# Convolution taps of six of eight value head pairs split over ScalarE, VectorE and GpSimd, with silu one pair of projections later

## The chip, the cores and the metric

The kernel runs on one core of one Trainium2 chip. The metric is the device time of one execution in microseconds (us). Five engines matter here, each with its own instruction queue that runs in order: TensorE (PE; its weight loads are shown as PEld), VectorE (DVE), ScalarE (ACT), GpSimd (POOL), and SyncE (SP), whose queue issues nearly all DMAs. GpSimd works on SBUF; results of matmuls lie in PSUM and are read by VectorE and ScalarE.

## The reference

The block is an adaptive layernorm around a gated delta-rule attention layer, followed by a mixture of experts. The input has 4 batches, 1024 tokens and 256 channels; the attention has 16 heads of 64 channels (C = 1024). Only the part that makes the values matters for this change; keys and queries are made in the same way.

```python
def _causal_conv(x, w, b):      # K = 4 taps per channel, causal
    y = jax.lax.conv_general_dilated(x, w, window_strides=(1,), padding=[(K - 1, 0)],
            feature_group_count=C, dimension_numbers=('NCH', 'OIH', 'NCH'))
    return y + b[None, :, None]
v = jnp.einsum('btd,cd->bct', hidden_states, Wv)
v = jax.nn.silu(_causal_conv(v, conv_v_w, conv_v_b))
...
def step(S, xs):                # a scan over the tokens
    kt, vt, qt, at, bt = xs
    v_old = jnp.einsum('bhij,bhj->bhi', S, kt)
    upd = vt - at[..., None] * v_old
    dS = upd[..., :, None] * kt[..., None, :]
    S = jnp.clip(at[..., None, None] * S + bt[..., None, None] * dS, -5.0, 5.0)
    ot = jnp.einsum('bhij,bhj->bhi', S, qt)
    return (S, ot)
...
g = jax.nn.silu(jnp.einsum('btd,cd->btc', hidden_states, Wg) + bg)
y = y * g
```

So each value channel is a projection of the normed rows, then o[t] = b + sum over j of w[j] * x[t + j - 3], then silu. The gate g is a second projection with a silu of its own, and multiplies the attention's output.

## The kernel before

All data is float32. The 1024 tokens are cut into 32 chunks of 32 tokens, and two chunks make a pair (class `Pair`). A tile of one head pair for one pair of chunks has 128 partitions (two heads of 64 channels) and 256 elements (2 chunks x 4 batches x 32 tokens); there are eight head pairs (HP = 8).

The main part is a software pipeline over the 16 pairs. While pair g's two chunks go through the recurrence (`passes`, L1098: state S, outputs, the output projection), pair g+1 is prepared: norm, decays, keys and queries, values and gates, the triangular system. Each of these jobs is a Python generator, and `work` (L1350) steps the generators in the order of the string `PLAN` (L59), one letter a step: `k` keys and queries, `v` values, `c` passes, `b` bounds, `d` decays, `t` triangle, `s` scaling, `r` routing, and so on; what is left of the generators after the string is run to its end in the order of the dictionary. The order in which the program is written out in this way is the order on PE, DVE, ACT and POOL (a hand-made schedule); semaphores between the engines are derived from what each instruction reads and writes. After the 16 pairs come the experts (`blocks`), from about 1600 us of the span on.

`values` (L760) makes, for each two head pairs (hp even): two projections of two matmuls each (`project`, L606, matmuls at L610) into two of three PSUM banks, which all short-lived products share in turn (`bank`, L401); ScalarE then writes tap 0 and the bias from PSUM to the tile `v` (L619). `convolve` (L624) adds taps 1, 2 and 3 on VectorE, one SCALAR_TENSOR_TENSOR each (L628), so six for the two head pairs; a bank is free when the third has read it. Then come the two gate projections (L780) with their silu on ScalarE into `gate` (L787), and, in the step after the second, the silu of the 512 elements of `v` (L634). These are six steps `v` for two head pairs, and 24 for a pair, as many as `PLAN` has.

Lines that the prediction's steps touch:

- L1231 (`decayed`): aS = S * last decay, on GpSimd, 128 x 1024, four times a pair of chunks; L1196 (`state`): S = ps_s + aS on VectorE.
- L1304, L1312, L1319 (`bounds`): on VectorE, a small product, a transpose, and two scans of 128 x 32 that read two tiles of SBUF.
- L726 (`decays`): two scans of 128 x 512 that read two tiles of SBUF; L705: sigmoid into ab_r on ScalarE, with a table load before it.
- L533 (`routing`): the matmul of the router, into a bank; L853 (`triangle`): the products of keys with keys and queries.
- L1001 (`scaled`): GpSimd multiplies keys and queries by a scale that a DMA brings; L1278: x1 = x1 + add on GpSimd; L934 to L956: VectorE's products and sums of the triangular inverse.
- L1019 (`below`): matmuls of the next step; L1252: yT = ps_y * gate on VectorE, which frees two banks.

The steps around the second value convolution stand in `PLAN` as `... c22 v7 v8 v9 c23 x c24 c25 c26 k28 b5 k29 c27 c28 b6 k30 r1 c29 ...` (the number says which step of its generator it is). c22 ends with L1196, v9 is the convolution of head pairs 2 and 3, c23 issues L1231, b5 is L1304 and L1312, b6 is the two L1319, k30 the last convolution of keys and queries, c29 the next L1196.

Of the kernel before, what the change touches and what calls it, by code (L numbers as in the profile page):

```python
# [36 lines left out]
ALU = mybir.AluOpType  # L37
# [3 lines left out]
B, D, C, NH, DH, KC = 4, 256, 1024, 16, 64, 4  # L41
HP = NH // 2
TC, TH, TE = 32, 16, 8
# [138 lines left out]
def adaln_block(ctx: ExitStack, tc: tile.TileContext, a: dict, out: bass.AP):  # L182
# [16 lines left out]
    n_safe = cst.tile([1, 3], I32, name="n_safe")  # L199
    rt = Routes(nc, cst, nch, con, ones, modt)  # L200
    chunks(tc, a, nch, con, ones, modt, modc, x1_dram, rt, out)
    blocks(tc, a, nch, con, rt, out)
    with tc.tile_pool(name="n_ps", bufs=1, space=PSUM) as pp:
# [158 lines left out]
def chunks(ctx, tc, a, nch, con, ones, modt, modc, x1_dram, rt, out):  # L362

    nc = tc.nc
# [16 lines left out]
    is_open, done = {}, set()  # L381

    def take(pool, shape, name, tag=None, bufs=1, **more):
        tag = tag or name
        assert is_open.get(tag, 0) < bufs, tag
        is_open[tag] = is_open.get(tag, 0) + 1
        if bufs > 1:
            more["bufs"] = bufs
        return pool.tile(shape, F32, name=name, tag=tag, **more)
# [6 lines left out]
    def need(*what):  # L396
        assert done.issuperset(what), what
# [3 lines left out]
    def bank(shape, name):  # L401
        banks[0] += 1
        return ps_g.tile(shape, F32, name=name, tag=f"g{banks[0] % 3}")
# [9 lines left out]
    QC, KK, VC = 0, 1, 2  # L413
# [17 lines left out]
    def load_v(hp):  # L431
        w = s3.tile([P, 2, P], F32, name="w_v", bufs=3)
        nc.sync.dma_start(w, a["w_qkv"][:, :, VC, hp])
        wg = s3.tile([P, 2, P], F32, name="w_gt", bufs=4)
        for p in range(2):
            nc.sync.dma_start(wg[:, :, half_p(p)], a["w_g"][:, :, p, hp * DH : (hp + 1) * DH])
        return w, wg
# [168 lines left out]
    def project(w, h_t, x, hp, o):  # L606

        ps = bank([P, 2 * B, KC - 1 + TC], "ps_q")
        for dc in range(2):
            nc.tensor.matmul(  # L610
                ps.rearrange("p y t -> p (y t)"),
                lhsT=w[:, dc],
                rhs=h_t[:, dc].rearrange("p x b t -> p (x b t)"),
                start=(dc == 0),
                stop=(dc == 1),
            )
        taps = conv[:, x, hp]
        o = o.rearrange("p x b t -> p (x b) t")
        nc.scalar.activation(  # L619
            o, ps[:, :, 0:TC], AF.Identity, scale=taps[:, 0:1], bias=taps[:, KC : KC + 1]  # L620
        )
        return ps, taps, o

    def convolve(*projected):  # L624

        for j in range(1, KC):
            for ps, taps, o in projected:
                nc.vector.scalar_tensor_tensor(  # L628
                    o, ps[:, :, j : j + TC], taps[:, j : j + 1], o, op0=ALU.mult, op1=ALU.add
                )  # L630

    def silu(f):
        f = f.rearrange("p h x b t -> p (h x b t)")
        nc.scalar.activation(f, f, AF.Silu)  # L634
# [5 lines left out]
    class Pair:  # L640
# [100 lines left out]
        def keys_and_queries(self):  # L741
            need(("h", self.g), ("halo", self.g))
            kq = self.kq = take(s2, [P, 2, HP, 2, B, TC], "kq", bufs=2)
            for hp in range(HP):
                w = w_next.pop(0)
                w_next.append(load_kq((hp + 2) % HP))
                two = []
                for x, i in ((KK, 0), (QC, 1)):
                    two.append(project(w[:, :, i], self.h_t, x, hp, kq[:, i, hp]))
                    yield  # L750
                convolve(*two)
                yield
                if hp % 2:
                    for i in range(2):
                        silu(kq[:, i, hp - 1 : hp + 1])
                        if i and hp == HP - 1:
                            done.add(("kq", self.g))
                        yield

        def values(self):  # L760

            need(("h", self.g), ("halo", self.g))
            self.v = []
            gate = self.gate = take(s2, [P, HP, 2, B, TC], "gate", bufs=2)
            for hp in range(HP):
                if hp % 2 == 0:
                    two, wgs = [], []
                    self.v.append(take(s2, [P, 2, 2, B, TC], "v", bufs=6))
                    for i in range(2):
                        w, wg = v_next.pop(0)  # L770
                        v_next.append(load_v((hp + i + 2) % HP))
                        wgs.append(wg)
                        two.append(project(w, self.h_t, VC, hp + i, self.v[-1][:, i]))
                        yield
                    convolve(*two)
                    yield
                wg = wgs[hp % 2]
                ps = bank([P, 2 * B, TC], "ps_gt")
                for dc in range(2):
                    nc.tensor.matmul(  # L780
                        ps,
                        lhsT=wg[:, dc],
                        rhs=self.h_t[:, dc, :, :, KC - 1 :].rearrange("p x b t -> p (x b) t"),
                        start=(dc == 0),
                        stop=(dc == 1),
                    )
                nc.scalar.activation(  # L787
                    gate[:, hp].rearrange("p x b t -> p (x b t)"),
                    ps.rearrange("p y t -> p (y t)"),
                    AF.Silu,  # L790
                    bias=b_gt[:, hp : hp + 1],
                )
                yield
                if hp % 2:
                    silu(self.v[-1])
                    if hp == HP - 1:
                        done.add(("v", self.g))
                    yield

        def rows_of_k(self):  # L800

            need(("kq", self.g), ("dec", self.g))
            kend = self.kend = []
            kmax = take(s1, [P, 32], "kmax")
            for par in range(2):
                kend.append(take(s3, [P, HP, 2, DH], "kend", bufs=3))
                for x in range(2):
                    need(("kq", self.g))
                    hs = slice(4 * x, 4 * x + 4)
                    ps = bank([P, 4, 2, DH], "ps_kt")  # L810
                    for i in range(4):
                        nc.tensor.transpose(
                            ps[:, i].rearrange("q p j -> q (p j)"),
                            self.kq[:, 0, 4 * x + i, par].rearrange("q b t -> q (b t)"),
                            ident,
                        )
                    pick = lambda z: z.rearrange("q (p x h) -> q x h p", p=2, x=2)[:, par, hs]
                    nc.vector.tensor_reduce(pick(kmax), ps, AX.X, ALU.max)
                    nc.vector.tensor_tensor(
                        kend[par][:, hs],  # L820
                        ps,
                        pick(self.dec[:, :, TC - 1]).unsqueeze(3).to_broadcast([P, 4, 2, DH]),
                        ALU.mult,
                    )
                    yield
            done.add(("kt", self.g))

            nc.vector.tensor_scalar_max(kmax, kmax, -SILU_MIN)
            self.k_twice = take(s2, [P, 2, 32], "k_twice", bufs=3)
            in_halves(self.k_twice, kmax)  # L830
            close("kmax")
            yield
            k_t = s1.tile([P, 2, TC], F32, name="k_t")
            nc.vector.transpose(
                k_t.rearrange("p x t -> p (x t)"), self.k_twice.rearrange("p x n -> p (x n)")
            )
            nc.sync.dma_start(of_pair(1, self.g), k_t.rearrange("p x t -> p (x t)"))
            yield
# [666 lines left out]
    for g in range(npair):  # L1505
# [4 lines left out]
        if g + 1 < npair:  # L1510
            x = newer
# [895 lines left out]
```

## Time and profile before

| what | us |
|---|---|
| median of three runs | 1913.18 |
| lowest and highest of them | 1906.1 and 1915.0 |
| the profiled execution, its own time | 1922.9 |
| its span, first to last instruction | 1921.1 |
| busy in the span: PE, DVE, ACT, POOL | 1632.0, 1482.3, 826.7, 716.4 |
| granted TensorE clock, mean over the span | 0.919 |
| one SCALAR_TENSOR_TENSOR of `v`, L628 (384 of them) | 0.476 |
| tap 0 of `v` on ACT, L619 (128 of them) | 0.573 |
| silu of `v` on ACT, L634 | 0.62 |
| one L1001 on POOL, 128 x 512 (128 of them) | 1.299 |
| one L1231 on POOL, 128 x 1024 (64 of them) | 1.914 |

The span is from the first to the last instruction of the profiled execution, which took 1922.9 us by its own measure; the medians come from other executions. In the stretch from 150 to 1420 us fourteen pairs of chunks go by, 90.7 us each; there PE is busy for 1132.5 of 1270 us, DVE for 1044.7, ACT for 613.5 and POOL for 493.2. Durations of single instructions include their start-up: instructions that follow each other on one engine overlap a little, so that six L628 in a row take 2.43 to 2.53 us and not 2.86.

### The profile page before, as it was taken

What the parts mean: (1) busy time and instruction counts of PE and PEld (TensorE: products, weight loads), DVE (VectorE), ACT (ScalarE), POOL (GpSimd) and SP (SyncE); (2) the same over time, 40 slices, a digit from 0 to 9 for tenths busy, and PEclk for the clock granted to TensorE, in tenths of its full rate; (3) what the DMA queues carried; (4) which work ended last, traced back from release to release, by engine and by line L of the source; (5) the groups of instructions that cost most, each with busy time, mean ns of one, the idle gap of its engine ahead of it and who ended that gap; (6) DMA issues with size and microseconds to landing.
All of it is one profiled execution on the core that took longest, in us unless ns stands there. A gap on an engine that the chain in (4) does not pass through costs nothing.

```text
span 1921.1 us, 88201 instructions
## 1 busy us (share of the span) xinstructions
PE 1632.0 (85%) x38610; PEld 1297.1 (68%) x38610; DVE 1482.3 (77%) x3622; ACT 826.7 (43%) x1652; POOL 716.4 (37%) x913
## 2 busy tenths in 40 slices
PE   5578999889989898989898989898888675989994
PEld 3456676667676766767676767676667564878883
DVE  4678797968788888878787978797968335789973
ACT  3344545444545544545445444554443112334331
POOL 1032343424342525252534343433424432454343
PEclk9889998989999998989899989998989677999997
DMA  4455444443545445354535453636343216788882
GB/s 117 127 161 129 105 108 94 107 109 95 148 115 141 123 120 137 107 134 111 146 103 150 106 153 97 161 94 153 110 112 112 56 36 207 187 208 219 231 231 35
DMA packets 431490, 249.52 MB, mean 130 GB/s; under 512 B 242996, under 2 KB 410808, under 8 KB 430840
## 3 DMA queue, kind: packets, MB, share of 16 engines
q1 hardware_dynamic: 416488, 223.65, 43.6%
q0 software_dynamic: 13664, 18.38, 5.2%
q8 instruction: 306, 5.01, 1.1%
q10 hardware_dynamic: 944, 1.77, 0.3%
q14 instruction: 88, 0.72, 0.1%
HBM read 165.99 MB, written 81.87 MB: 129 GB/s over the span
## 4 chain that ended last, share of the span: by engine, by line
PE 66%; DVE 11%; issue 7%; POOL 5%; SPq 5%; DMA 4%; ACT 3%; POOLq 0%; DVEq 0%; ACTq 0%
PE ps_q L610 22%; PE ps_hm L2116 6%; PE ps_yb L2129 6%; PE ps_w L1265 5%; PE ps_gt L780 4%; PE ps_u L1149 3%; PE ps_kk L853 3%; PE ps_o L1208 2%; PE ps_z L1127 2%; SPq L423 2%; PE ps_t L1031 2%; PE ps_s L1187 2%; DMA sc<-g_scratch 2%; PE ps_t L1019 2%; DVE kq L628 2%
## 5 line engine op out<-in xcount | busy, mean ns | idle before, releaser
L628 DVE SCALAR_TENSOR_TENSOR kq<-ps_q,w_conv,kq 128x256 f32<-128x256 f32 x768 | 319.7, 476 | 150.2 <-ACT kq L619 149.6
L610 PE MATMUL ps_q<-hT,w_kq 128*128 128x280 f32 x1024 | 323.2, 460 | 58.9 <-issue 20.6
L610 PEld LDWEIGHTS ps_q<-hT,w_kq 128*128 128x128 f32 x1024 | 203.5, 213 | 125.9 <-issue 58.2
L619 ACT ACTIVATE kq<-ps_q,w_conv 128x256 f32<-128x256 f32 x256 | 142.4, 563 | 234.8 <-PE ps_q L610 233.1
L1001 POOL TENSOR_TENSOR kq<-kq,sc 128x512 f32<-128x512 f32 x128 | 163.5, 1299 | 143.6 <-DMA sc<-g_scratch 116.5
L2136 POOL DMA_INDIRECT out<-yb,at_b x72 | 120.4, 1672 | 190.2 <-DVE gate L2106 48.7
L628 DVE SCALAR_TENSOR_TENSOR v<-ps_q,w_conv,v 128x256 f32<-128x256 f32 x384 | 158.9, 476 | 41.9 <-ACT v L619 41.7
L1231 POOL TENSOR_TENSOR aS<-S,last 128x1024 f32<-128x1024 f32 x64 | 122.5, 1914 | 135.9 <-DVE S L1196 133.4
L780 PE MATMUL ps_gt<-hT,w_gt 128*128 128x256 f32 x512 | 144.3, 410 | 29.6 <-issue 20.5
L787 ACT ACTIVATE gate<-ps_gt,b_gt 128x256 f32<-128x256 f32 x128 | 60.5, 473 | 239.3 <-PE ps_gt L780 239.1
L610 PE MATMUL ps_q<-hT,w_v 128*128 128x280 f32 x512 | 153.5, 441 | 11.6 <-issue 4.7
L2116 PE MATMUL ps_hm<-hT,w 128*128 128x256 f32 x576 | 136.4, 392 | 7.6 <-issue 5.9
L2123 ACT ACTIVATE hm<-ps_hm,b 128x256 f32<-128x256 f32 x144 | 68.2, 474 | 167.5 <-issue 120.4
L2129 PE MATMUL ps_yb<-w,hm 128*128 128x256 f32 x576 | 130.3, 379 | 0.0
L2116 PEld LDWEIGHTS ps_hm<-hT,w 128*128 128x128 f32 x576 | 112.7, 197 | 25.9 <-issue 8.9
L610 PEld LDWEIGHTS ps_q<-hT,w_v 128*128 128x128 f32 x512 | 97.7, 204 | 47.3 <-issue 13.1
L780 PEld LDWEIGHTS ps_gt<-hT,w_gt 128*128 128x128 f32 x512 | 92.0, 194 | 53.1 <-issue 28.5
L1265 PE MATMUL ps_w<-w_o,yT 128*128 128x256 f32 x512 | 121.0, 391 | 4.3 <-DVE yT L1252 2.8
L1278 POOL TENSOR_TENSOR x<-x,add 128x256 f32<-128x256 f32 x32 | 29.0, 905 | 236.4 <-DVE add L1276 232.3
L2129 PEld LDWEIGHTS ps_yb<-w,hm 128*128 128x128 f32 x576 | 106.7, 190 | 13.4 <-DVE yb L2134 0.3
L1265 PEld LDWEIGHTS ps_w<-w_o,yT 128*128 128x128 f32 x512 | 98.2, 195 | 20.1 <-DVE yT L1252 3.0
L619 ACT ACTIVATE v<-ps_q,w_conv 128x256 f32<-128x256 f32 x128 | 71.3, 573 | 93.7 <-PE ps_q L610 93.7
(265 smaller groups left out, 3230.5 us busy)
## 6 DMA issues: line engine op xcount, KB each, us to landing
w<-in_w SPq DMA_DIRECT2D x72, 512.0 KB
rows_scratch<-zero_row SPq DMA_DIRECT2D x272, 132.0 KB
w_kq<-in_w_qkv SPq DMA_DIRECT2D x260, 128.0 KB
sc<-g_scratch SPq DMA_DIRECT2D x128, 256.0 KB
w_v<-in_w_qkv SPq DMA_DIRECT2D x130, 128.0 KB
w_gt<-in_w_g SPq DMA_DIRECT2D x260, 64.0 KB
u_scratch<-u SPq DMA_DIRECT2D x128, 128.0 KB
hb<-rows_scratch SPq DMA_DIRECT2D x36, 264.0 KB
```

The lines of the kernel that those rows point to most:

```text
L610: nc.tensor.matmul(ps.rearrange("p y t -> p (y t)"), lhsT=w[:, dc], rhs=h_t[:, dc].rearrange("p x b t -> p (x b t)"), start=(dc == 0), sto ...
L619: nc.scalar.activation(o, ps[:, :, 0:TC], AF.Identity, scale=taps[:, 0:1], bias=taps[:, KC : KC + 1])
L628: nc.vector.scalar_tensor_tensor(o, ps[:, :, j : j + TC], taps[:, j : j + 1], o, op0=ALU.mult, op1=ALU.add)
L780: nc.tensor.matmul(ps, lhsT=wg[:, dc], rhs=self.h_t[:, dc, :, :, KC - 1 :].rearrange("p x b t -> p (x b) t"), start=(dc == 0), stop=(dc == 1),
L787: nc.scalar.activation(gate[:, hp].rearrange("p x b t -> p (x b t)"), ps.rearrange("p y t -> p (y t)"), AF.Silu, bias=b_gt[:, hp : hp + 1],)
L1001: nc.gpsimd.tensor_tensor(o, o, sc[:, h4 : h4 + 4], ALU.mult)
L1231: nc.gpsimd.tensor_tensor(aS.rearrange("q b h i -> q (b h) i"), S[:, bs].rearrange("q b h i -> q (b h) i"), self.pair.last[self.par][:, bs ...
L1265: nc.tensor.matmul(ps_w, lhsT=self.yT[:, hp].rearrange("q b t -> q (b t)"), rhs=w_o[:, hp], start=(hp == 0), stop=(hp == HP - 1),)
L2116: nc.tensor.matmul(ps, lhsT=self.w1[:, dc, fc * P : (fc + 1) * P], rhs=self.hT[:, dc], start=(dc == 0), stop=(dc == 1),)
L2123: nc.scalar.activation(self.hm[:, fc], ps, AF.Gelu, bias=self.b1[:, fc : fc + 1])
L2129: nc.tensor.matmul(ps, lhsT=self.hm[:, fc, s * P : (s + 1) * P], rhs=self.w2[:, fc], start=(fc == 0), stop=(fc == 3),)
L2136: return nc.gpsimd.indirect_dma_start(out=places, out_offset=bass.IndirectOffsetOnAxis(ap=self.at[:, s : s + 1], axis=0), in_=y, in_offset ...
```

## The change

For head pairs 0 to 5 (hp = 0, 2, 4) the four taps are made on two engines: ScalarE writes tap 0 and the bias into `v` as before, and then tap 1 into a second place, `more`, with a second instruction (`half_taps`); VectorE adds taps 2 and 3 to `more`, two instructions for each head pair in place of three; GpSimd adds `more` to `v`, one instruction of 128 x 512 for two head pairs. `more` is the place of the gates of the next two head pairs in the tile `gate`, which is written by its own silu later. The last two head pairs (hp = 6) stay as they were.

The silu of `v` moves: where that of head pairs 2 and 3 stood, that of 0 and 1 is issued, and so on; the first place is empty, and that of the last two head pairs is issued in a 25th step, after the end of `PLAN`. In a pair of chunks there are six more instructions on ACT, six fewer on DVE, and three more on POOL. No DMA and no matmul is added, removed or moved.

```diff
-    def convolve(*projected):
-
-        for j in range(1, KC):
+    def convolve(*projected, first=1):
+
+        for j in range(first, KC):
             for ps, taps, o in projected:
                 nc.vector.scalar_tensor_tensor(
                     o, ps[:, :, j : j + TC], taps[:, j : j + 1], o, op0=ALU.mult, op1=ALU.add
                 )
+
+    def half_taps(w, h_t, hp, o, more):
+
+        ps, taps, o = project(w, h_t, VC, hp, o)
+        nc.scalar.mul(more, ps[:, :, 1 : 1 + TC], taps[:, 1:2])
+        return ps, taps, more
...
-                        two.append(project(w, self.h_t, VC, hp + i, self.v[-1][:, i]))
+                        o = self.v[-1][:, i]
+                        if hp + 2 < HP:
+                            more = gate[:, hp + 2 + i].rearrange("p x b t -> p (x b) t")
+                            two.append(half_taps(w, self.h_t, hp + i, o, more))
+                        else:
+                            two.append(project(w, self.h_t, VC, hp + i, o))
                         yield
-                    convolve(*two)
+                    if hp + 2 < HP:
+                        convolve(*two, first=2)
+                        flat = lambda z: z.rearrange("p h x b t -> p (h x b t)")
+                        o = flat(self.v[-1])
+                        nc.gpsimd.tensor_tensor(o, o, flat(gate[:, hp + 2 : hp + 4]), ALU.add)
+                    else:
+                        convolve(*two)
                     yield
...
                 if hp % 2:
-                    silu(self.v[-1])
-                    if hp == HP - 1:
-                        done.add(("v", self.g))
+                    if hp > 1:
+                        silu(self.v[-2])
                     yield
+            silu(self.v[-1])
+            done.add(("v", self.g))
+            yield
```

## The prediction

> **What bounds the kernel now.** I read the page first, then the waits of the stretch from 150 to 1420 us (fourteen of the fifteen pairs that run beside a recurrence), then the timelines of each engine over the pair that begins at 843 us. The page's first table and its chain of waits:
>
> ```profile
> PE 1632.0 (85%) x38610; PEld 1297.1 (68%) x38610; DVE 1482.3 (77%) x3622; ACT 826.7 (43%) x1652; POOL 716.4 (37%) x913
> ...
> PE 66%; DVE 11%; issue 7%; POOL 5%; SPq 5%; DMA 4%; ACT 3%; POOLq 0%; DVEq 0%; ACTq 0%
> ```
>
> PE carries two thirds of the chain, DVE a ninth. So time saved on DVE counts only where PE stands and waits for DVE. The waits of the stretch name such places:
>
> ```profile
> DVE S L1196 <- POOL aS L1231: 15.4, 10, 2.9
> ...
> PE ps_q L610 <- DVE yT L1252: 14.5, 9, 2.8
> ...
> PE ps_t L1019 <- ACT ab_r L705: 12.0, 11, 1.1
> ...
> PE ps_l L533 <- DVE kq L628: 3.2, 13, 0.2
> ```
>
> The columns are us in total, times, longest. Line 2 is the end of a pair: PE waits for yT, which stands behind the last L1196 on DVE, and that waits for GpSimd's aS (line 1) in ten pairs, 4 to 13. Line 4 is small, but it happens in every pair. PE is at the convolution's heels there, so any delay of that convolution is a delay of PE.
>
> **The three convolutions that change**, for the pair at 843 us. In a queue that is full, L628 follows L628 every 0.394 us (five take 2.05, and the last 0.475: (2.05 - 0.475) / 4). Two fewer save DVE 0.79 us. The new ACT instruction is nearest to L2102 of the experts, a multiply of 128 x 256 by a column, 0.497 us; L619 with a bias column takes 0.573. I take 0.50, of which 0.40 follows an instruction before it.
>
> First (863.9 to 867.5 us). ACT's two instructions for the two heads start 0.95 us apart, as PE delivers them. The new one fits behind the first, but the second head's ends at 865.79, so DVE, which is not late here, ends at 867.10 instead of 867.47. What follows waits for ACT's tap 0 of kq at 868.96, as before. ACT's copies of z come 0.40 later; PE, busy until 866.31, waits under 0.2 us for them and had 0.29 idle just behind. Worth: 0, within 0.2 us.
>
> Third (908.9 to 914.3). DVE is late here (it starts at 911.89, ACT ended at 910.45), so the full 0.79 us is saved, and then stands as idle time in front of the last L1196, which waits 0.89 us for aS already. aS comes from a queue of SP's DMAs and GpSimd work that the change leaves alone. Worth: 0 in pairs 4 to 13.
>
> Second. This one decides. DVE's, then GpSimd's, then PE's timeline of it:
>
> ```profile
> 885.65 1.21 DVE L1196 TENSOR_TENSOR S<-ps_s,aS 128x1024 f32<-128x1024 f32 x1
> 886.79 2.53 DVE L628 SCALAR_TENSOR_TENSOR v<-ps_q,w_conv,v 128x256 f32<-128x256 f32 x6
> 889.24 0.21 DVE L1304 TENSOR_TENSOR grow<-most,k_twice 128x64 f32<-128x64 f32 x1
> 889.48 0.25 DVE L1312 STREAM_TRANSPOSE grow_t<-grow 128x64 f32<-128x64 f32 x1
> 889.76 0.46 DVE L1319 TENSOR_TENSOR_SCAN peak<-a_t,peak,grow_t 128x32 f32<-128x32 f32 x2
> 890.14 0.46 DVE L628 SCALAR_TENSOR_TENSOR kq<-ps_q,w_conv,kq 128x256 f32<-128x256 f32 x1
> 890.84 2.05 DVE L628 SCALAR_TENSOR_TENSOR kq<-ps_q,w_conv,kq 128x256 f32<-128x256 f32 x5 [0.24 <-ACT kq L619]
> ```
>
> ```profile
> 886.95 1.90 POOL L1231 TENSOR_TENSOR aS<-S,last 128x1024 f32<-128x1024 f32 x1 [7.27 <-DVE S L1196]
> ```
>
> ```profile
> 892.65 0.58 PE L533 MATMUL ps_l<-w_router,hT 128*128 128x8 f32 x4 [0.25 <-DVE kq L628]
> ```
>
> The columns are start, length, engine, line. Today aS runs beside the convolution. In the new order the GpSimd add of step v9 stands in front of aS (step c23) in GpSimd's queue, and it waits for the convolution. ACT's second head ends at 887.23, the new tap at 887.63, then three L628: the convolution ends at 888.95, 0.37 earlier. GpSimd starts 0.09 us after DVE ends (as aS after L1196 here: 886.86, 886.95), at 889.04. The add of 128 x 512 is nearest to L1001, also two plain tiles, whose least is 1.25: it ends at 890.3. Then aS, 1.90, until 892.2. The next L1196 starts at 892.81, so aS is not late by itself. But GpSimd is now busy from 889.04 to 892.2, and DVE's L1319 falls into that.
>
> **What GpSimd does to such DVE instructions** is in the trace, from another place of the same pair (DVE, GpSimd) and from pair 2 (DVE, GpSimd):
>
> ```profile
> 875.78 0.97 DVE L1319 TENSOR_TENSOR_SCAN peak<-a_t,peak,grow_t 128x32 f32<-128x32 f32 x2
> ```
>
> ```profile
> 875.94 0.73 POOL L1278 TENSOR_TENSOR x<-x,add 128x256 f32<-128x256 f32 x1 [15.00 <-DVE add L1276]
> ```
>
> ```profile
> 276.96 0.48 DVE L943 TENSOR_TENSOR X<-X,rk 128x64 f32<-128x64 f32 x1
> 277.47 1.94 DVE L948 TENSOR_TENSOR prod<-T,X 128x512 f32<-128x512 f32 x1
> ```
>
> ```profile
> 276.08 2.51 POOL L1001 TENSOR_TENSOR kq<-kq,sc 128x512 f32<-128x512 f32 x2 [4.25 <-DMA sc<-g_scratch]
> ```
>
> Two L1319 take 0.46 alone and 0.97 here: the second ends at 876.75, just after L1278's end at 876.67. It stood still for all of it. L943 (0.22 alone) waits for the first L1001 and slips in between the two; L948 (1.04 alone) then waits for the whole second one. Both read two tiles of SBUF. L628, which reads PSUM, lies beside GpSimd's work with no change (0.474 with, 0.475 without). The scan L726 takes 1.62 beside aS and 1.21 alone, so aS blocks scans too.
>
> So the first L1319 (ready at about 889.4) waits for the add until 890.3 and slips in; aS is ready and goes next; the second L1319 waits for aS and ends at about 892.35. The convolution of kq, which reads PSUM but is behind it in DVE's queue, starts at 892.27 instead of 890.14. Its fifth instruction frees the bank of L533: 892.27 + 4 x 0.394 + 0.475 = 894.32, before it was 892.50. **The price is 1.82 us of PE in a pair**, and PE has no other idle time there (0.25 before, all on this wait). All fifteen pairs show the same order and the same 0.25: 15 x 1.82 = 27.3 us.
>
> Bounds of this price. From below: both scans run between add and aS, and only the add is in the way; the convolution then starts at 890.54, the bank is free at 892.59, and the price is 0.1 us. From above: in pairs 3 and 14 a waiting L943 got no turn at all through five GpSimd instructions and lasted 4.91 us instead of 0.22. If both scans wait until GpSimd is idle (aS, then L549 and L561, some 0.6 more), the price is 2.6 us, 39 us in all. I take 1.82, as three such places (pairs 1, 2, 15) show one turn and then a loss.
>
> The Trainium skill's "SBUF — State Buffer" (section "SBUF: two separate sides") says that the pair of ports shared by DVE and GpSimd is a lock: whichever starts first holds it for its whole instruction. The rows above show this, but pair 3 does not: there L943 started at 368.17, aS at 368.37, and L943 still waited until 373.08. By the rule the sum is the 27 us above; by that row it is the 39.
>
> **The rest, all pairs.** The silu of `v` moves. No DMA goes with it, and the first empty place saves ACT time where it was idle. At the end of a pair two silus stand where one stood, in front of L705's table load: two in a row take 1.15, one 0.62, so ab_r comes 0.53 later, and L1019 with it (PE already waits 1.09 for it). In pairs 5 to 13 PE idles 0.57 to 2.8 us for yT just behind, which hides it. In pairs 1 to 4 and 14 that idle time is under 0.1: 5 x 0.53 = 2.6 us. Before the first recurrence (pair 0) the chain runs through DVE: its second and third convolutions win 0.3 and 0.8, but each add then blocks a two-tile DVE instruction for some 1.0: +1 us. The silu now waits for GpSimd's add, which ends over 10 us before; the gates overwrite `more` more than 10 us after it.
>
> Sum: 27.3 + 2.6 + 1 = 31 us. The profiled execution took 1922.9 (span 1921.1), so 1954 for one like it. The median of the runs is 1913.2, 9.7 under it; against that, **1944 us**.
>
> **Rivals.**
> 1. The scans slip through (the lower bound), or never meet the add: 15 x 0.1 + 2.6 + 1 = 5, or 2.6 - 1 = 2 without any blocking. 1915 to 1918. For it: L943 did slip in between two GpSimd instructions. Against it: the second of two L1319 lost to L1278 when GpSimd was ready 0.03 us before it. Chance 0.28.
> 2. Faster: DVE's relief is paid. From 902 to 932 us DVE hardly rests; if it, and not aS, were the last to reach the final L1196, the third convolution's 0.79 would reach PE in each pair: 15 x 0.79 = 12, 1901. It decides from the point where the idle time before that L1196 is 0, which is so in pairs 1 to 3, 14 and 15, and not in the ten others (0.89 to 2.9 us). Chance 0.10.
> 3. The forecast, from 0.9 us a pair up to the 39 us, and some 6 more if PE's new idle time of 2 us brings stretches at half the granted clock, as around 934 us, where PE idles 1.09 and 1.05 us and the clock reads 0.50. 1930 to 1962. Chance 0.62.
>
> A measurement of this kernel tells about 0.5% from no change, some 10 us: faster 0.10, same 0.28, slower 0.62. The range 1911 to 1962 holds cases 1 and 3.
>
> **What would show it.** L1319 at the second convolution: 0.46 for two, now 2.5 or more. L533's wait for L628: 0.25 a pair, now about 2. aS (L1231) of that place starting after an add. L1019's wait for ab_r 1.6 instead of 1.09. DVE's busy time falls by 96 x 0.39 = 38 us in L628 and gains more than 15 x 1.8 in L1319. Wrong if the two L1319 stay under 1.5 us, or if aS there still starts ahead of the add.

## The result and the profile after

| what | before | after |
|---|---|---|
| median, lowest to highest, us (four runs each) | 1913.62, 1906.1 to 1915.0 | 1939.38, 1936.82 to 1942.38 |
| ratio after / before, 95% interval | | 1.0143 [1.0113, 1.0174] |
| profiled execution: time, span, us | 1922.9, 1921.1 | 1938.8, 1937.0 |
| granted clock, mean over the span | 0.919 | 0.909 |

The change costs 1.4%, some 26 us (22 to 33 by the interval); the forecast was 1944, 31 us above before. The ratio, here and below, leaves out a few slow executions, so it can differ a little from the quotient of two medians. The two profiled executions are 15.9 us apart only; that of before is 9 us above its median. Lines from `values` on carry numbers that are 19 higher in the new kernel: L1338 is the scan L1319, L1250 is aS (L1231), L1215 is L1196, L1323 is L1304, L1038 is L1019. L711 is the sigmoid into ab_r (L705) and L732 the scan L726. New are L635, ScalarE's tap 1, and L790, GpSimd's add; `more` is a place in the tile `gate`, so the taps that go there carry that name. The first table and the chain of waits of the page after:

```profile
PE 1633.9 (84%) x38610; PEld 1307.8 (68%) x38610; DVE 1502.9 (78%) x3526; ACT 860.4 (44%) x1748; POOL 789.9 (41%) x961
...
PE 61%; DVE 16%; issue 6%; SPq 5%; DMA 5%; POOL 4%; ACT 3%; POOLq 0%; DVEq 0%; ACTq 0%
```

DVE has 96 instructions fewer and is busy 20.6 us longer; its share of the chain goes from 11% to 16%. Work was taken off it, and time was put on it. The groups of instructions say where: L628 for values falls from 158.9 us to 82.3 + 39.1, so by 37.5, and the scans rise from 22.8 (399 ns each) to 59.8 (976 ns). Most of the rest is in the products of the triangular inverse, L939 (L920 before), which had 26.8 us and now have 41.6. The waits of the stretch from 150 to 1440 us, in the same columns as those of before:

```profile
POOL v L790 <- DVE grow L1323: 132.3, 13, 18.4
...
PE ps_l L533 <- DVE kq L628: 25.8, 13, 2.3
...
PE ps_t L1038 <- ACT ab_r L711: 16.0, 10, 1.6
...
DVE S L1215 <- POOL aS L1250: 12.1, 8, 2.3
```

L533 waited 3.2 us in these pairs and now waits 25.8. The wait for ab_r went from 12.0 to 16.0, 1.09 to 1.6 at a time. The first line is GpSimd's own idle time and costs nothing; the last, the wait for aS, was 15.4 before.

The second convolution in the pair that begins at 852 us, DVE's timeline, then GpSimd's, then PE's:

```profile
899.53 1.27 DVE L628 SCALAR_TENSOR_TENSOR gate<-ps_q,w_conv,gate 128x256 f32<-128x256 f32 x3 [0.37 <-ACT gate L635]
900.72 0.22 DVE L1323 TENSOR_TENSOR grow<-most,k_twice 128x64 f32<-128x64 f32 x1
...
901.25 2.90 DVE L1338 TENSOR_TENSOR_SCAN peak<-a_t,peak,grow_t 128x32 f32<-128x32 f32 x2
904.08 2.41 DVE L628 SCALAR_TENSOR_TENSOR kq<-ps_q,w_conv,kq 128x256 f32<-128x256 f32 x6
```

```profile
900.95 1.26 POOL L790 TENSOR_TENSOR v<-v,gate 128x512 f32<-128x512 f32 x1 [9.37 <-DVE grow L1323]
902.17 1.90 POOL L1250 TENSOR_TENSOR aS<-S,last 128x1024 f32<-128x1024 f32 x1
```

```profile
906.24 0.58 PE L533 MATMUL ps_l<-w_router,hT 128*128 128x8 f32 x4 [1.96 <-DVE kq L628]
```

Read the three by their ends. The add ends at 902.21, aS at 904.07, and at 904.08 the next convolution begins: DVE's two scans, 0.46 us before, last 2.90, until 904.15, just past the end of aS. The bank comes free late, and PE's 0.25 has become 1.96. The scans do this in all fifteen pairs (one has 3.22, and 2.27 at L533). The first pair has no router yet; there PE waits for the same convolution at L872 (L853 before), 2.24 us instead of 0.53, again 1.71 more. So 15 x 1.71 = 25.7 us.

Not all of it stays: PE's time without work, the span less PE's busy time, grows from 289.1 to 303.1 us in the two profiled executions, by 14.0 only. Some waits elsewhere became shorter, that for yT (table below) from 14.6 to 7.8.

### The profile page after: what moved, and what is told of

It is laid out like the page before. It is cut to its first block, busy times and chain, and to the rows that moved or that the text cites. A ratio compares the mean times of both kernels' runs of the same rounds, so it can differ in the third digit from the quotient of the medians.

```text
span 1937.0 us, 88489 instructions
## 1 busy us (share of the span) xinstructions
PE 1633.9 (84%) x38610; PEld 1307.8 (68%) x38610; DVE 1502.9 (78%) x3526; ACT 860.4 (44%) x1748; POOL 789.9 (41%) x961
## 4 chain that ended last, share of the span: by engine, by line
PE 61%; DVE 16%; issue 6%; SPq 5%; DMA 5%; POOL 4%; ACT 3%; POOLq 0%; DVEq 0%; ACTq 0%
PE ps_q L610 19%; PE ps_hm L2135 6%; PE ps_yb L2148 6%; PE ps_w L1284 4%; PE ps_gt L797 4%; PE ps_kk L872 3%; PE ps_u L1168 3%; DVE peak L1338 2%; DMA sc<-g_scratch 2%; DVE kq L628 2%; SPq L423 2%; PE ps_z L1146 2%; PE ps_t L1050 2%; PE ps_t L1038 2%; PE ps_s L1206 2%
## 5 line engine op out<-in xcount | busy, mean ns | idle before, releaser
L628 DVE SCALAR_TENSOR_TENSOR kq<-ps_q,w_conv,kq 128x256 f32<-128x256 f32 x768 | 318.5, 475 | 143.4 <-ACT kq L619 141.0
L610 PE MATMUL ps_q<-hT,w_kq 128*128 128x280 f32 x1024 | 316.1, 451 | 47.5 <-issue 15.5
L790 POOL TENSOR_TENSOR v<-v,gate 128x512 f32<-128x512 f32 x48 | 73.6, 1533 | 274.6 <-DVE grow L1323 141.6
L610 PE MATMUL ps_q<-hT,w_v 128*128 128x280 f32 x512 | 150.9, 434 | 11.7 <-issue 4.6
L1250 POOL TENSOR_TENSOR aS<-S,last 128x1024 f32<-128x1024 f32 x64 | 123.0, 1922 | 5.9 <-DVE S L1215 3.4
L628 DVE SCALAR_TENSOR_TENSOR gate<-ps_q,w_conv,gate 128x256 f32<-128x256 f32 x192 | 82.3, 477 | 46.9 <-ACT gate L635 46.9
L2125 DVE SCALAR_TENSOR_TENSOR gate<-gates,share,gate 128x256 f32<-128x256 f32 x216 | 104.4, 483 | 6.5 <-ACT gate L2121 1.4
```

Source lines behind the costliest of these rows:

```text
L610: nc.tensor.matmul(ps.rearrange("p y t -> p (y t)"), lhsT=w[:, dc], rhs=h_t[:, dc].rearrange("p x b t -> p (x b t)"), start=(dc == 0), sto ...
L628: nc.vector.scalar_tensor_tensor(o, ps[:, :, j : j + TC], taps[:, j : j + 1], o, op0=ALU.mult, op1=ALU.add)
L790: nc.gpsimd.tensor_tensor(o, o, flat(gate[:, hp + 2 : hp + 4]), ALU.add)
L1250: nc.gpsimd.tensor_tensor(aS.rearrange("q b h i -> q (b h) i"), S[:, bs].rearrange("q b h i -> q (b h) i"), self.pair.last[self.par][:, bs ...
L2125: nc.vector.scalar_tensor_tensor(self.gate[:, s], gates[:, b], self.share[:, s, b : b + 1], self.gate[:, s], op0=ALU.mult, op1=ALU.add,)
```

## The experiments

The theory: GpSimd's add and aS, run back to back beside two DVE scans that read two SBUF tiles, hold each scan up for one GpSimd instruction; a convolution queued behind the scans passes that on to PE. The rivals: the added work itself (the longer ACT queue, GpSimd's load), or the silu's move. The table holds all runs; each ratio is against runs of the kernel before on the same chip (medians 1926.9 for e1 to e4, 1924.1 for e5 to e8, 1914.9 for e9 to e11, 1916.7 for e12), with its 95% interval. The last columns are from the traces: length of the two scans of the second convolution and PE's wait at L533 there, per pair, and PE's idle time summed over the fifteen pairs in front of L1019 (ab_r) and of the next convolution's matmuls behind it (yT). These sums count all idle time at the place, whichever releaser the profile names, so they are larger than the lines of the waits.

| kernel | ratio | scans | L533 | ab_r | yT |
|---|---|---|---|---|---|
| before | 1 | 0.46 | 0.25 | 14.3 | 14.6 |
| after | 1.0143 [1.0113, 1.0174] | 2.90 | 1.96 | 20.3 | 7.8 |
| e1_silu | 1.0047 [1.0018, 1.0076] | 0.46 | 0.25 | 21.7 | 12.0 |
| e2_second_whole | 1.0001 [0.9972, 1.0031] | 0.46 | 0.25 | 21.0 | 9.0 |
| e3_add_later | 1.0015 [0.9981, 1.0048] | 0.46 | 0.25 | 21.1 | 8.7 |
| e4_extra_add | 1.0188 [1.0144, 1.0232] | 2.61 | 2.06 | 13.5 | 11.3 |
| e5_scans_last | 1.0003 [0.9964, 1.0042] | 0.45 | 0.25 | 23.2 | 7.4 |
| e6_two_adds | 1.0107 [1.0067, 1.0146] | 1.75 | 1.20 | 17.6 | 11.9 |
| e7_write_only | 1.0076 [1.0038, 1.0114] | 2.10 | 1.15 | 21.6 | 4.5 |
| e8_old_silu | 0.9988 [0.9948, 1.0027] | 0.46 | 0.25 | 14.6 | 7.6 |
| e9_two_memsets | 0.9993 [0.9960, 1.0026] | 0.46 | 0.25 | 21.1 | 7.2 |
| e10_early_silu | 0.9936 [0.9904, 0.9969] | 0.46 | 0.25 | 12.9 | 11.1 |
| e11_before_early | 0.9986 [0.9953, 1.0019] | 0.46 | 0.25 | 11.3 | 11.8 |
| e12_third_whole | 0.9962 [0.9925, 0.9998] | 0.46 | 0.25 | 12.7 | 11.7 |

### One part alone: the silu's move

The kernel before with the last part of the diff:

```diff
                 if hp % 2:
-                    silu(self.v[-1])
-                    if hp == HP - 1:
-                        done.add(("v", self.g))
+                    if hp > 1:
+                        silu(self.v[-2])
                     yield
+            silu(self.v[-1])
+            done.add(("v", self.g))
+            yield
```

> The kernel before, with the silu of v moved one pair of projections later and nothing else. Theory (the scans L1319 stand between two GpSimd instructions at the second convolution): +2.6 us from L1019's later start in pairs 1 to 4 and 14, within 0 to +5; L533 still waits 0.25 us a pair. Rival (the later silus and ScalarE's order make the loss): most of the 26 us, +18 or more.

Measured: 1935.66 against 1926.87, +9 us (by the interval, +3.5 to +14.6). The scans and L533 are untouched, so this is not the price at L533. Its waits:

```profile
PE ps_t L1021 <- ACT ab_r L705: 16.0, 10, 1.6
PE ps_q L610 <- DVE yT L1254: 11.8, 6, 2.9
```

ab_r is late by half a us in nearly every pair (sum 14.3 to 21.7), and PE's idle time for yT, which was to absorb it, shrinks by 2.6 only. The two together make +4.8 us. The two profiled spans are 13.2 us apart (1934.3 and 1921.1), and 9.2 of that is PE's busy time (1641.2 against 1632.0), at a granted clock of 0.911 instead of 0.919. Whether the later ab_r brings the lower clock about was not tried; e5's profile has the same clock and PE busy for 1643.6 us in a span of 1920.9. So 4.8 us of the 9 have a shown place, and the interval does not demand more.

### The change without its second split, and with the second add later

e2: the change with head pairs 2 and 3 whole on DVE.

```diff
-                        if hp + 2 < HP:
+                        if hp in (0, 4):
...
-                    if hp + 2 < HP:
+                    if hp in (0, 4):
```

> The changed kernel, with all three taps of head pairs 2 and 3 on VectorE again, so that the first and third convolutions alone are split. Theory: the whole price sits at the second, so this is 0 to +6 us against the kernel before, and L533 waits 0.25 us a pair again. Rival (each split costs its share, by ScalarE's and GpSimd's added work): two thirds of 26, +17 us.

e3: all three splits, the add of head pairs 2 and 3 issued one step later, which puts it behind aS and the scans.

```diff
                         o = flat(self.v[-1])
-                        nc.gpsimd.tensor_tensor(o, o, flat(gate[:, hp + 2 : hp + 4]), ALU.add)
+                        if hp != 2:
+                            nc.gpsimd.tensor_tensor(o, o, flat(gate[:, hp + 2 : hp + 4]), ALU.add)
                     else:
                         convolve(*two)
                     yield
+                    if hp == 2:
+                        nc.gpsimd.tensor_tensor(o, o, flat(gate[:, hp + 2 : hp + 4]), ALU.add)
```

> The changed kernel with all taps split as there, but GpSimd's add of head pairs 2 and 3 is issued one step of its generator later, behind the two scans and behind aS in GpSimd's queue. Theory: L1319 takes 0.5 us for two again, L533 waits 0.25, and the time is 0 to +6 us against the kernel before. Rival (ScalarE's second tap makes the convolution late, or GpSimd's added work as such): +20 or more, as in the changed kernel.

Measured: 1927.62 and 1930.01; neither can be told from the kernel before. In both the scans take 0.46 again (1.22 in the first pair of e3, and of e8, e10 and e12, which are made from it) and L533 waits 0.25. e3 has every instruction of the change, the extra ACT tap and the extra add included; only the add's place differs. So the price is the place. Against the change itself, e3's ratio is lower by 0.0128, some 24.6 us, where the trace counts 25.7.

### The suspected cost put into the kernel before

e4: one GpSimd instruction that nothing needs, in the add's place.

```diff
                     convolve(*two)
+                    if hp == 2:
+                        flat = lambda z: z.rearrange("p h x b t -> p (h x b t)")
+                        o = flat(self.v[-1])
+                        nc.gpsimd.tensor_tensor(flat(gate[:, hp + 2 : hp + 4]), o, o, ALU.add)
                     yield
```

> The kernel before, with one added GpSimd instruction per pair of chunks: v + v of head pairs 2 and 3 into the free place in gate, where the changed kernel has its second add; nothing reads it. No tap, no silu is moved. Theory: two L1319 take some 2.9 us, L533 waits 1.9 to 2.3 us a pair, +24 to +32 us (here the convolution ends 0.37 later than in the changed kernel). Rivals (silu, ScalarE): 0 to +3.

e6: the same with two of them in a row, the second into the gates of the next two head pairs.

```diff
-                        nc.gpsimd.tensor_tensor(flat(gate[:, hp + 2 : hp + 4]), o, o, ALU.add)
+                        for z in (gate[:, hp + 2 : hp + 4], gate[:, hp + 4 : hp + 6]):
+                            nc.gpsimd.tensor_tensor(flat(z), o, o, ALU.add)
```

> The kernel before with two GpSimd adds (not one) of 128 x 512, one after the other, behind the second convolution; nothing reads what they write (two places of gate that are overwritten later). Compare with e4_extra_add, which has one such add. Theory of one turn (a DVE instruction that waits gets in between two GpSimd instructions, the next one waits for the whole GpSimd instruction that follows): the first scan goes in after the first add, the second after the second add, aS is no longer waited for; two scans take about 2.0 us instead of 2.61, L533 waits about 1.4 instead of 2.06, and the kernel is some 5 to 10 us faster than e4_extra_add although it does more work. Rival 1 (the waiting is for all of GpSimd's queue): 1.25 us more a pair, L533 about 3.3, some 19 us slower than e4_extra_add. Rival 2 (what counts is aS only): the same as e4_extra_add.

The scans in e4 (DVE), and GpSimd beside them:

```profile
900.19 2.61 DVE L1323 TENSOR_TENSOR_SCAN peak<-a_t,peak,grow_t 128x32 f32<-128x32 f32 x2
```

```profile
899.82 1.04 POOL L779 TENSOR_TENSOR gate<-v 128x512 f32<-128x512 f32 x1 [9.70 <-DVE v L628]
900.82 1.90 POOL L1235 TENSOR_TENSOR aS<-S,last 128x1024 f32<-128x1024 f32 x1
```

The same in e6:

```profile
897.79 1.75 DVE L1324 TENSOR_TENSOR_SCAN peak<-a_t,peak,grow_t 128x32 f32<-128x32 f32 x2
```

```profile
897.43 2.03 POOL L780 TENSOR_TENSOR gate<-v 128x512 f32<-128x512 f32 x2 [9.73 <-DVE v L628]
899.42 1.90 POOL L1236 TENSOR_TENSOR aS<-S,last 128x1024 f32<-128x1024 f32 x1
```

One add makes +36 us (e4; 28 to 45 by the interval, where 24 to 32 were expected). 1.81 at L533 x 15 = 27 of them are in the trace, and the rest is unexplained; the granted clock of e4's runs is 0.902 on average, that of before 0.919, and what part the clock has in the time was not tried. With one more the scans end at 899.54, with the second add at 899.46, and not with aS at 901.32: more GpSimd work, a shorter stall. L533 waits 1.20 instead of 2.06, and the ratio is 0.008 lower, some 15 us; the two intervals just touch, so the wait in the trace carries the verdict, and the times agree with it. The rival of a wait for all of GpSimd's queue asked for 3.3 at L533 and falls; so does the one that counts aS alone.

### The consumer moved: scans behind the convolution

The change with two neighbouring steps of `PLAN` exchanged:

```diff
- c23 x c24 c25 c26 k28 b5 k29 c27 c28 b6 k30 r1
+ c23 x c24 c25 c26 k28 b5 k29 c27 c28 k30 b6 r1
```

> The kernel after with two neighbouring steps of the written order exchanged: the six DVE instructions of the second kq convolution go ahead of the step that ends in the two scans L1338. The GpSimd add stays ahead of aS. Theory (the price is two scans that GpSimd holds back, with a convolution queued behind them): the convolution no longer stands behind the scans, PE's wait at L533 falls from 1.96 us to about 0.25, the scans meet only the tail of aS (both in under 1.5 us), and the kernel is within 0 to +10 us of the kernel before (the silu's share). Rival (the price is GpSimd's or ACT's extra work itself, by whatever way it meets DVE): L533 still waits 1 us or more and the time stays about 25 us above the kernel before.

Measured: 1925.11, ratio 1.0003. The add and aS still run back to back (894.03 to 897.17 in the pair looked at), but DVE reads PSUM meanwhile, and the scans follow at 897.78 with 0.45. L533 is back at 0.25. So the add in its first place costs nothing that can be measured once the scans are not due beside it.

### Is it GpSimd's reading?

e7: e3 with a memset in the add's old place, made to wait for the convolution (`last`, its last instruction, is returned by `convolve`).

```diff
                         if hp != 2:
                             nc.gpsimd.tensor_tensor(o, o, flat(gate[:, hp + 2 : hp + 4]), ALU.add)
+                        else:
+                            zero = nc.gpsimd.memset(flat(gate[:, hp + 4 : hp + 6]), 0.0)
+                            behind(tc, zero, last)
```

> e3_add_later (the change with its second add behind the scans) with a GpSimd memset of 128 x 512 where the add stood in the change: it waits for the convolution, writes a place of gate that is overwritten later, and reads nothing; nothing reads it. Theory A (DVE instructions of two SBUF operands are held back by GpSimd instructions that read SBUF): the memset holds nothing back, the scans stay near 0.46 for two or meet only aS (one of them up to 1.9), the kernel is within 6 us of e3_add_later unless aS is pushed onto the scans. Theory B (any GpSimd instruction on SBUF holds them back, reading or not): two scans 2 us or more, L533 1 to 2 us, 15 to 27 us above e3_add_later. If the memset delays aS so that a scan meets aS alone, L533 lies between and the first scan's own duration decides between A and B.

e9: the same with two memsets.

```diff
+                            zero = nc.gpsimd.memset(flat(gate[:, hp + 4 : hp + 6]), 0.0)
+                            behind(tc, zero, last)
```

> e7_write_only with two such memsets in a row (0.52 us each there) ahead of aS: more GpSimd work still. In e7 the first scan ran beside the memset's end in 0.28 us (its length alone), the second met aS and took 1.89, and L533 waited 1.15. Theory A (a GpSimd instruction that only writes holds no scan back): both scans run beside the second memset and are over before aS begins; 0.46 for two, L533 0.25, and the time comes down to that of e3_add_later, about 14 us of PE under e7_write_only. Theory B (any GpSimd instruction holds them): the first scan goes in behind a memset, the second behind the next one or behind aS; two scans 0.9 us or more, L533 0.8 to 2 us.

e7, DVE and GpSimd:

```profile
898.47 2.10 DVE L1345 TENSOR_TENSOR_SCAN peak<-a_t,peak,grow_t 128x32 f32<-128x32 f32 x2
```

```profile
898.09 0.52 POOL L792 MEMSET gate<- 128x512 f32 x1 [9.28 <-DVE gate L628]
898.57 1.92 POOL L1257 TENSOR_TENSOR aS<-S,last 128x1024 f32<-128x1024 f32 x1
```

e9, DVE and GpSimd:

```profile
881.81 0.46 DVE L1347 TENSOR_TENSOR_SCAN peak<-a_t,peak,grow_t 128x32 f32<-128x32 f32 x2
```

```profile
881.42 0.52 POOL L792 MEMSET gate<- 128x512 f32 x1 [9.27 <-DVE gate L628]
882.00 0.53 POOL L794 MEMSET gate<- 128x512 f32 x1
882.49 1.90 POOL L1259 TENSOR_TENSOR aS<-S,last 128x1024 f32<-128x1024 f32 x1
```

In e7 the memset is over before it can tell much; it pushes aS onto the second scan, which alone costs 0.9 us at L533. In e9 the scans (881.81 to 882.27) run beside the two memsets (881.42 to 882.53), at their undisturbed length, and are over before aS starts at 882.49. Ratio 0.9993 against 1.0076, L533 0.25 against 1.15: a second useless instruction took the stall away. Theory A holds, as far as one kind of write-only instruction can show it. The Trainium skill's "SBUF — State Buffer" (section "Who interferes with whom") says the same: a DVE instruction with two SBUF inputs contends with a GpSimd instruction that reads SBUF, and not with one that only writes it.

### Towards a better version

e8: e3 with the silu in the places of the kernel before.

```diff
                 if hp % 2:
-                    if hp > 1:
-                        silu(self.v[-2])
+                    silu(self.v[-1])
+                    if hp == HP - 1:
+                        done.add(("v", self.g))
                     yield
-            silu(self.v[-1])
-            done.add(("v", self.g))
-            yield
```

> e3_add_later with the silu of v in the places of the kernel before; the rest of the change stays, the second add behind the scans. Theory (the silu's move alone costs some 9 us through L1038's wait for ab_r, the first and third split give some 6 back): PE's wait before L1038 falls from 1.6 to about 1.1 us a pair, and the time is 4 to 9 us under e3_add_later, so 0 to 6 us under the kernel before. Rival (ACT's later silu has nothing to do with it, the 9 us of e1 come from the state of the clock): the same as e3_add_later. Risk: a silu of the second head pair now waits for the late add, on ACT, and holds back ACT's gate or tap 0 behind it; then L610's idle time grows.

e10 is e8, e11 the kernel before, each with this edit:

```diff
+                if hp == HP - 1:
+                    silu(self.v[-1])
                 wg = wgs[hp % 2]
...
                 if hp % 2:
-                    silu(self.v[-1])
+                    if hp < HP - 1:
+                        silu(self.v[-1])
```

> e8_old_silu (the splits of the change, the second add behind the scans, silu in the old places) with the last silu of v taken one place forward, ahead of the last gate L807 on ACT: ACT stands idle there for 0.4 to 2.3 us. A candidate for a version faster than both kernels. Theory (ab_r is last on PE's path at the end of a pair, so ACT time there is PE time; the other way round from e1_silu): L1038's wait for ab_r falls from 1.09 to 0.5 to 0.7 us, the time by 4 to 8 us against e8_old_silu, to 2 to 13 us under the kernel before. Rival (yT, behind aS, sets the end of a pair, and PE only waits there instead): the wait for ab_r falls, L610's wait for yT grows by the same, time as e8_old_silu.

> The kernel before with nothing changed but the place of the last silu of v: ahead of the last gate L787 on ACT. The mirror of e1_silu, which put a second silu in front of ab_r and cost 9 us. Theory: L1019's wait for ab_r falls from 1.09 to 0.5 to 0.7 us in each pair, and the time by 4 to 8 us. Rival (yT behind aS takes its place): PE's idle time before L610 grows from 14.6 us in sum by as much as the wait for ab_r loses (7 us), and the time stays within 3 us of the kernel before.

e8 measured 1919.42, ratio 0.9988: as expected in size, but not to be told from the kernel before. ab_r's wait fell to 14.6 in sum, as the theory had it. e10 measured 1905.20, **0.9936 [0.9904, 0.9969]: faster than both kernels**, by 12 us against before as the ratio has it. ACT's timeline at the end of one of its pairs:

```profile
829.09 0.63 ACT L640 ACTIVATE v<-v 128x512 f32<-128x512 f32 x1 [0.47 <-DVE v L628]
829.90 0.47 ACT L809 ACTIVATE gate<-ps_gt,b_gt 128x256 f32<-128x256 f32 x1 [0.18 <-PE ps_gt L802]
...
832.00 0.22 ACT L711 ACTIVATE ab_r<-ps_ab 128x64 f32<-128x64 f32 x1 [0.33 <-PE ps_y L1270]
```

The silu now fills time in which ACT waited for the gate's matmuls, and ab_r waits for PE, no longer for ACT. Yet the sums of idle time tell the rival's story: e10's wait for ab_r falls by 1.7 us against e8, and its wait for yT grows by 3.5. The gain against before is measured; against e8 the two intervals overlap, so how much of it the silu's place brings is open, and its cause is not shown. For e11 the sums fall by 5.8 us and the time by an amount that cannot be told from none. In both, the wait for ab_r fell less than expected, to 0.86 and 0.75 us a pair.

### Is the third split worth anything?

e12: e10 with head pairs 4 and 5 whole on DVE.

```diff
-                        if hp + 2 < HP:
+                        if hp in (0, 2):
...
-                    if hp + 2 < HP:
+                    if hp in (0, 2):
```

> e10_early_silu with the third split taken back: the taps of head pairs 4 and 5 are all on DVE again, with no GpSimd add there. Why: with the split, six L628 become four (0.79 us saved), but the products L943 of the triangular inverse behind them, which read two SBUF tiles, take 41.6 us in the kernel instead of 26.8 before, 0.96 us a pair, because aS and the add run back to back beside them. Theory (the third split gives DVE nothing: 0.79 saved, 0.96 lost): L943's group is back at about 26.8, PE's idle time for yT and ab_r stays within 3 us of e10's 24.0 in sum, and the time is that of e10 within 0.5%. Rival (DVE's relief at the third convolution is what shortens PE's wait for yT at the end of a pair, as e2 against e1 seems to say): PE's wait for yT grows by 5 us or more in sum, and the time by 5 to 8 us against e10.

The products of the inverse in the kernel after, behind the third convolution of the pair at 852 us, GpSimd beside them, and their group over the whole run:

```profile
929.91 0.54 DVE L939 TENSOR_TENSOR prod<-wA,T 128x100 f32<-128x100 f32 x1
...
930.77 0.97 DVE L939 TENSOR_TENSOR prod<-wA,T 128x144 f32<-128x144 f32 x1
```

```profile
928.43 1.90 POOL L1250 TENSOR_TENSOR aS<-S,last 128x1024 f32<-128x1024 f32 x1
930.29 1.28 POOL L790 TENSOR_TENSOR v<-v,gate 128x512 f32<-128x512 f32 x1
```

```profile
L939 DVE TENSOR_TENSOR prod<-wA,T 128x4 f32<-128x4 f32 (+6 forms) x112 | 41.6, 371 | 2.3
```

The group in e12:

```profile
L943 DVE TENSOR_TENSOR prod<-wA,T 128x4 f32<-128x4 f32 (+6 forms) x112 | 26.9, 240 | 2.3
```

The two instructions of DVE take 0.26 and 0.31 us before. The first now ends at 930.45, with aS at 930.33, the second at 931.74, with the add at 931.57: the same turn for turn as at the second convolution. DVE gains 0.79 us at the third convolution and loses 0.94 behind it. With the split gone the group is back at 26.9, PE's idle time is the same (12.7 + 11.7 against 12.9 + 11.1), so by PE's waits the rival falls: the split gives DVE nothing here. The two times would not decide it. They agree within their intervals, but the ratios are 0.0026 apart, some 5 us, which is also the least that the rival asked for.

## Why the prediction was right

**The second convolution.** Right in mechanism, in place and nearly in size. Forecast: an add of 1.25 us, the first scan in between, aS next, the second scan until aS ends, 1.82 us a pair. Measured: 1.71. (The forecast's "all fifteen pairs" at L533 are fourteen; in the first pair it is L872 that waits.) The lower bound (0.1, scans slip through) and the upper one (2.6, both wait for an idle GpSimd) both fell: in all fifteen pairs the first scan took one turn and the second lost one. e3 and e5 show that it is the order alone, e4 and e6 that each scan waits for one instruction, e7 and e9 that a memset, which only writes, holds no scan back. The starved L943 of before's pairs 3 and 14 (4.91 us through five GpSimd instructions), from which the upper bound came, was not tried and stays open.

**The durations.** ACT's new tap 0.466 us (forecast 0.50). L628 -37.5 us (38). The add 1.26 us there (1.25), but 1.533 on average; the reason is the last section's.

**The silu's move: mis-sized.** The step that failed, in e1, is "in pairs 5 to 13 PE idles 0.57 to 2.8 us for yT just behind, which hides it": it counted five exposed pairs, 2.6 us. e1 cost 9 us, at least 3.5. The wait for ab_r is 1.6 in nearly all pairs, and yT's idle time gave back only 2.6 us in sum. What I took as fixed, the time at which aS and so yT come, moves with PE: in e1 DVE's wait for aS did not shrink when PE came later, it grew from 15.4 to 21.5 us in sum. Why it grew was not tried. In the change itself that wait is 12.1, the wait for ab_r grew by 6.0 and yT's idle time fell by 6.8, so there the two balance, and no price of the silu's move is seen.

**First and third convolution: "worth 0".** The third is worth 0 by PE's waits, but not for the forecast's reason. "The full 0.79 us is saved, and then stands as idle time" is wrong: the working stopped at the convolution, and the add and aS take 0.94 us back from two products a little later (e12). The forecast held the rule that would have found it, and applied it to the second convolution and to pair 0 only. Whether the first is worth anything stays open: e2 (first, third and the silu's move) is at 1.0001 and e1 (the move alone) at 1.0047, 8 us apart with intervals that overlap, and PE's idle time for yT is 3.0 us lower (6.8 lower in the change than in before). No run has the first split alone.

**The sum.** 25.7 us for the second convolution and 9 for the silu (3.5 to 14.6) make 34.7; measured were 26. So the terms do not simply add: in the change itself ab_r and yT cancel, and PE's time without work grew by 14.0 us only. That the forecast's 31 lies within 22 to 33 is in part luck. The place of the price does not rest on the sum: with the second split, the second add or the scans moved (e2, e3, e5), the time cannot be told from that of before. The +1 us of pair 0 cannot be checked: the first pair's scans begin at 154.4 us before and at 155.9 after, and between 150.9 and 158.9 in the experiments.

**Rivals.** Rival 1 (scans slip through) is what the kernel does once order or kind of GpSimd's instruction is changed (e3, e5, e9), not in the change as it stands. Rival 2 (DVE's relief is paid in every pair) fell for the third convolution. The extra time that the third case has for stretches at a low clock is open: the granted clock did fall, from 0.919 to 0.909, but PE's busy time grew by 1.9 us only.

## What to carry to other kernels

Before GpSimd is given an instruction that reads SBUF, list what DVE has due during it **and during the GpSimd instruction behind it** that reads two SBUF tiles, and what stands behind that on DVE; here the added instruction's own length was the smaller part of the price, since it also pushed the next one onto new victims. The remedy here was one step of order: the same work, one place later, cost nothing that could be measured. And idle time that stands behind another wait has to be checked as cover in the new trace: for the same later ab_r it shrank by 2.6 us in e1 and by 6.8 in the change.

## What the runs showed that was not expected

**The same conflict the other way round.** The add of the first convolution takes 2.05 us, not 1.26, in all pairs. DVE and GpSimd there, in the new kernel:

```profile
879.17 1.21 DVE L732 TENSOR_TENSOR_SCAN gam<-arep,eye 128x512 f32<-128x512 f32 x1
880.30 0.46 DVE L628 SCALAR_TENSOR_TENSOR kq<-ps_q,w_conv,kq 128x256 f32<-128x256 f32 x1
```

```profile
879.40 2.05 POOL L790 TENSOR_TENSOR v<-v,gate 128x512 f32<-128x512 f32 x1 [4.93 <-ACT kq L619]
```

DVE's scan had begun 0.23 us earlier; it keeps its 1.21, and the add's last 1.07 us come after the scan's end at 880.38. It costs nothing there, since nobody waits for the add.

**More work on GpSimd made the kernel faster, twice**: e6 against e4 (two adds for one: the scans 1.75 us instead of 2.61), e9 against e7 (two memsets for one: 0.46 instead of 2.10). The times bear the second out clearly; for the first, the two intervals just touch. What counts is which instruction is running when the DVE instruction comes up, and where it ends.
